# A macaron block with a selective scan: feed-forward stages dealt out in 128-token tiles, 3 or 4 beside each scan step

## The chip, the cores and the metric

The kernel runs on one core of a Trainium2 chip. A core has five engines with an instruction queue each, which meet through semaphores: TensorE (PE; its weight loads are shown as PEld), VectorE (DVE), ScalarE (ACT), GpSimd (POOL) and SyncE (SP), which here issues nearly all DMAs. The metric is device time in microseconds for one execution, as the median of several runs.

## What is computed

The input x has 4 sequences of 1024 tokens with 512 features, all float32. Three blocks follow each other, each with a layer normalisation in front of it and a residual around it: a feed-forward block (halved), a selective scan, and the same feed-forward block once more.

```python
x = x + 0.5 * ffn(layernorm(x))
x = x + attn(layernorm(x))
x = x + 0.5 * ffn(layernorm(x))

def ffn(x):                      # INTER = 1408
    g = einsum('th,ih->ti', x, gate_w) * gate_s
    u = einsum('th,ih->ti', x, up_w) * up_s
    return einsum('ti,hi->th', silu(g) * u, down_w) * down_s

def attn(x):                     # I = 1024 channels, N = 16 states, R = 128
    h, gate = split(einsum('blh,oh->bol', x, W_in), 2)
    h = silu(causal_conv4(h) + conv_b)
    ts, B, C = split(einsum('bil,oi->blo', h, Wx), [R, R + N])
    ts, B, C = rms(ts), rms(B), rms(C)
    delta = softplus(einsum('blr,ir->bil', ts, Wdt) + dt_bias)
    # s = exp(delta * A) * s + delta * B * h;  y = sum over N of s * C
    y = (scan(h, delta, A, B, C) + D * h) * silu(gate)
    return einsum('bil,hi->blh', y, Wout)
```

## The kernel before

The 4096 tokens are cut into 16 chunks of T = 256 tokens (J = 2 tiles of 128), four to a sequence. A chunk passes three stages: the first feed-forward pass (x to x1 in DRAM), the scan (x1 to x2 in DRAM), the second feed-forward pass (x2 to the output).

**The scan is the spine.** Step k scans chunk k. It has NI = 8 tiles of 128 channels with NS = 4 units each, 32 units in all. A unit (`unit`, L517) works on two halves of 2 x 256 columns: ACT computes the decay `da` into PSUM (L533), POOL the input `sb` (L536), DVE scans (L540) and multiplies by C into `pr` (L546), and ACT saves the last state (L545). One unit later PE adds up `pr` over the states into `yps` (`add_up`, L553). `da` has four buffers (two units), `sb` four (two units), `pr` three (three units). For every two channel tiles `head` (L448) makes delta with two small `dp` matmuls and ACT's `z`, `lg` (L461 to L469), POOL finishes it (`rest`, L472 to L476), and `rows` and `spread` send it through DRAM so that each row stands on 32 partitions.

**Everything else is background**, a list of `Work` pieces, each with a cost in PE columns, which `background(k)` (L656) makes for each step. The loop at L738 emits a unit, and after it as many pieces as keep the share of PE work done level with the share of DVE work; the pieces up to the next chunk's parameters are to be done HEAD = 10 units before the step's end. Weights come through a ring of 15 blocks of 256 KB, loaded up to LEAD = 13 blocks ahead in the order in which the pieces use them (`fetch`, L110). The queues' final order is a scheduler's; pinned instructions keep the order of the program.

In the background of step k stand: the gate half of W_in for chunk k (`gate`, L498: PE matmuls `gp`, ACT copies to `g`, one silu), the output projection of chunk k-1 (`tail`, L574: `op`, 32 records of 128x512), normalisation and transposes of chunk k+1 (`flips`), its conv half of W_in (`prep_conv`, L345: `hp`), its parameters (`prep_params`, L378: `sp`, `t`, `tsT`), and one **feed-forward pass** (class FFN, L212) over up to four tiles: 11 `gate_w` blocks, 11 `up_w` blocks, one `fo` group of 11 down matmuls for each 128-token tile. A float32 matmul shows as two records in the trace.

**What decides which tokens go where** is L638 to L643:

```python
    beside = {0: [(1, 1), (1, 2)]}
    for k in range(1, NCS):
        beside[k] = ([(1, k + 2)] if k + 2 < NCS else []) + ([(2, k - 2)] if k >= 2 else [])
    beside[NCS - 2].append((2, NCS - 3))
    beside[NCS - 1] = [(2, NCS - 2)]
```

An entry is (pass, chunk), so 256 tokens. Step 0 has two entries (512 tokens), step 1 one, steps 2 to 14 two, step 15 one. The first pass of chunk 0 is done alone in front (`start`), the second pass of chunk 15 alone at the end (`end`, L713): it loads x2 from DRAM after `tail` has stored it. Steps 14 and 15 are `late` (L645): their last entry is the chunk whose scan has just ended, so they do the tail first, and load and flip that chunk inside the step.

In front of the scan (L708 to L711) stand the first pass of chunk 0, the flips of step 0's pass and of chunk 0, `prep_conv(0)` with `gate(0)` woven in piece by piece, and the parameters with the first gate blocks of step 0's pass.

Of the kernel before, what the change touches and what calls it, by code (L numbers as in the profile page):

```python
# [13 lines left out]
P = 128  # L14
# [18 lines left out]
LEAD = 13  # L33
RING = 15
# [3 lines left out]
def macaron_kernel(ctx: ExitStack, tc: tile.TileContext, a: dict, out: bass.AP):  # L38
# [173 lines left out]
    class FFN:  # L212


        def __init__(self, name, halves):
            self.name, self.halves = name, halves
            self.n = len(halves) * T
            self.x = {}

        def load(self, h):  # L220
            if self.halves[h][0] == 2:
                settle()
                write()
            stage, c = self.halves[h]
            for j in range(J):
                r = c * J + j
                t = self.x[h, j] = p8.tile([P, H], F32, tag="xf", name=f"xf{self.name}_{h}_{j}")
                load(out=t, in_=a["x"][r * P : (r + 1) * P, :] if stage == 1 else x2[r])

        def stats(self, h, j):  # L230
            return stats(self.x[h, j], f"f{self.name}_{h}_{j}")

        def flip(self, xn, h, j):
            if not hasattr(self, "xT"):
                self.xT = p1.tile([P, KH, 2 * T], F32, tag="fxT", name=f"fxT{self.name}")
            o = h * T + j * P
            flip(xn, self.xT[:, :, o : o + P], f"f{self.name}_{h}_{j}")
# [42 lines left out]
        def down(self):  # L280
            parts = [(h, j) for h in range(len(self.halves)) for j in range(J)]
            wd = []

            def part(h, j):
                def emit(w=None):
                    wd.extend(w or [])
                    nm = f"{self.name}_{h}_{j}"
                    op = ps_m.tile([P, H], F32, tag="mm", name=f"fo{nm}")
                    o = h * T + j * P
                    for it in range(NF):  # L290
                        nc.tensor.matmul(  # L291
                            op, lhsT=self.hd[:, it, o : o + P], rhs=wd[it],
                            start=(it == 0), stop=(it == NF - 1),
                        )
                    x = self.x[h, j]
                    tmp = p2.tile([P, H], F32, tag="tmp", name=f"tmp{nm}")
                    stage, c = self.halves[h]
                    r = c * J + j
# [11 lines left out]
                return Work(NF * H, H, emit, [("down_w", it) for it in range(NF)] if h + j == 0 else ())  # L310

            r = [part(h, j) for h, j in parts]
# [261 lines left out]
    def tail(k):  # L574
# [3 lines left out]
        def part(j):  # L578
            def emit(w=None):
# [10 lines left out]
                store(x2[k * J + j], x)  # L590
# [15 lines left out]
    def flips(f, prep, halves=None):  # L606

        seq = []
        if f:
            seq = [(h, j) for h in (range(len(f.halves)) if halves is None else halves) for j in range(J)]  # L610
# [4 lines left out]
        def begin(n):  # L615
            if n < len(seq):
                h, j = seq[n]
                xn[n] = prep_stats(prep, j) if h is None else f.stats(h, j)
# [5 lines left out]
        def part(n):  # L624
            def emit():
                h, j = seq[n]
# [18 lines left out]
    def late(k):  # L645

        return k >= NCS - 2
# [208 lines left out]
```

## Time and profile before

| what | value |
|---|---|
| median of 3 runs | 3403.47 us (3403.05 to 3404.28) |
| the profiled execution: its time, its span | 3408.67 us, 3406.6 us |
| POOL L536, the scan's `sb` | 1024 x 1273 ns, 1280.4 us busy |
| DVE L540, the scan with a state | 1536 x 739 ns, 1060.1 us busy |
| ACT L533, the scan's `da` | 2048 x 470 ns, 901.3 us busy |
| DVE L546, `pr` | 1024 x 677 ns, 667.4 us busy |
| PE L243, `up_w` and `gate_w` | 1408 records each, 607.0 and 608.5 us busy |
| PE L291, `fo` | 1320 records, 587.4 us busy |
| PE L505 and L354, `gp` and `hp` | 1024 records each, 248.7 and 244.2 us busy |
| weight loads of gate, up, down | 198 each of 256 KB |
| DMA engines, mean busy share | 53.3% on the queue of SP's transfers |

Times are microseconds from the first instruction. The page's first part gives each engine's busy time; the second cuts the span into 40 slices, a digit being tenths of busy time, with the granted TensorE clock below. A stretch's row gives its length, and for each engine its busy time and (x) its instructions. A row of waits gives the waiting engine and instruction, what released it, and the total, the number and the longest of the waits. A busy engine is not an engine that sets the time: what matters is whether it has idle time, and what ended it.

### The profile page before, as it was taken

What the parts mean: (1) busy time and instruction counts of PE and PEld (TensorE: products, weight loads), DVE (VectorE), ACT (ScalarE), POOL (GpSimd) and SP (SyncE); (2) the same over time, 40 slices, a digit from 0 to 9 for tenths busy, and PEclk for the clock granted to TensorE, in tenths of its full rate; (3) what the DMA queues carried; (4) which work ended last, traced back from release to release, by engine and by line L of the source; (5) the groups of instructions that cost most, each with busy time, mean ns of one, the idle gap of its engine ahead of it and who ended that gap; (6) DMA issues with size and microseconds to landing.
All of it is one profiled execution on the core that took longest, in us unless ns stands there. A gap on an engine that the chain in (4) does not pass through costs nothing. (4 is left out here: it accounts for less than half of the span.)

```text
span 3406.6 us, 41741 instructions
## 1 busy us (share of the span) xinstructions
PE 3156.1 (93%) x12448; PEld 1609.4 (47%) x12448; DVE 2434.9 (71%) x4202; ACT 2001.4 (59%) x4395; POOL 2034.4 (60%) x1959
## 2 busy tenths in 40 slices
PE   8897676999999999999999999999999999989898
PEld 5534352544444454444445454444545444344445
DVE  1177686687868778786877778687786779757781
ACT  2446654756656575766657475765747576465551
POOL 1266655566665756666575666757566576655760
PEclk9997787999999999999999999999999999999899
DMA  6345454546555554656565465556546555643643
GB/s 201 97 125 138 136 137 123 147 129 185 146 163 156 155 156 117 189 138 171 142 171 161 118 180 137 161 142 171 163 124 177 130 161 142 186 114 100 192 136 105
DMA packets 286417, 504.59 MB, mean 148 GB/s; under 512 B 31984, under 2 KB 50160, under 8 KB 286192
## 3 DMA queue, kind: packets, MB, share of 16 engines
q1 hardware_dynamic: 284608, 501.47, 53.3%
q8 instruction: 100, 1.64, 0.2%
q14 instruction: 125, 1.02, 0.1%
q10 hardware_dynamic: 1584, 0.45, 0.1%
HBM read 442.56 MB, written 59.24 MB: 147 GB/s over the span
## 5 line engine op out<-in xcount | busy, mean ns | idle before, releaser
L536 POOL TENSOR_TENSOR sb<-rep,bc 128x512 f32<-128x512 f32 x1024 | 1280.4, 1273 | 466.0 <-DVE da L540 441.5
L540 DVE TENSOR_TENSOR_SCAN da<-da,state,sb 128x256 f32<-128x256 f32 x1536 | 1060.1, 739 | 263.5 <-ACT da L533 203.4
L533 ACT ACTIVATE da<-rep,a_w 128x256 f32<-128x256 f32 x2048 | 901.3, 470 | 266.2 <-DVE pr L546 249.4
L546 DVE TENSOR_TENSOR pr<-da,bc 128x512 f32<-128x512 f32 x1024 | 667.4, 677 | 77.8 <-ACT state L545 61.8
L243 PE MATMUL up_w<-fxT,w_up_w 128*128 128x512 f32 (+1 forms) x1408 | 607.0, 578 | 18.7 <-issue 13.7
L243 PE MATMUL gate_w<-fxT,w_gate_w 128*128 128x512 f32 (+1 forms) x1408 | 608.5, 577 | 9.6 <-ACT hd L257 4.8
L291 PE MATMUL fo<-w_down_w,hd 128*128 128x512 f32 x1320 | 587.4, 597 | 0.0
L556 PE MATMUL yps<-pr,fold 128*32 128x256 f32 x4096 | 386.6, 401 | 140.0 <-DVE pr L546 117.7
L545 ACT COPY state<-da 128x2 f32<-128x2 f32 x768 | 118.9, 161 | 498.6 <-DVE da L540 490.5
L243 PEld LDWEIGHTS up_w<-fxT,w_up_w 128*128 128x128 f32 x1408 | 260.5, 192 | 304.4 <-issue 288.3
L243 PEld LDWEIGHTS gate_w<-fxT,w_gate_w 128*128 128x128 f32 x1408 | 265.5, 193 | 283.8 <-issue 250.7
L540 DVE TENSOR_TENSOR_SCAN da<-da,sb 128x256 f32<-128x256 f32 x512 | 321.1, 679 | 96.5 <-ACT da L533 69.8
L291 PEld LDWEIGHTS fo<-w_down_w,hd 128*128 128x128 f32 x1320 | 244.6, 191 | 291.3 <-issue 282.7
L556 PEld LDWEIGHTS yps<-pr,fold 128*32 128x32 f32 x4096 | 105.0, 109 | 481.8 <-DVE pr L546 225.7
L472 POOL TENSOR_SCALAR e<-z 128x512 f32<-128x512 f32 x64 | 124.4, 1944 | 214.0 <-ACT z L468 204.9
L505 PE MATMUL gp<-mxT,w_W_in 128*128 128x256 f32 x1024 | 248.7, 392 | 1.9 <-ACT dd L467 1.1
L354 PE MATMUL hp<-mxT,w_W_in 128*128 128x259 f32 x1024 | 244.2, 388 | 5.7 <-issue 2.0
L585 PE MATMUL op<-w_Wout,u 128*128 128x512 f32 x512 | 234.6, 606 | 8.1 <-POOL sb L536 5.3
L365 DVE SCALAR_TENSOR_TENSOR u<-hp,conv_w,u 128x256 f32<-128x256 f32 x384 | 175.1, 473 | 71.2 <-ACT u L358 67.7
L354 PEld LDWEIGHTS hp<-mxT,w_W_in 128*128 128x128 f32 x1024 | 190.0, 190 | 62.3 <-issue 25.3
L505 PEld LDWEIGHTS gp<-mxT,w_W_in 128*128 128x128 f32 x1024 | 190.7, 192 | 57.2 <-issue 21.8
L566 POOL TENSOR_TENSOR u<-u,g 128x256 f32<-128x256 f32 x128 | 92.8, 730 | 196.4 <-DVE u L562 196.2
(114 smaller groups left out, 2744.5 us busy)
## 6 DMA issues: line engine op xcount, KB each, us to landing
rep<-row SPq DMA_DIRECT2D x512, 256.0 KB, 5.6
w_W_in<-in_W_in_dram SPq DMA_DIRECT2D x256, 256.0 KB, 3.1
w_gate_w<-in_gate_w_dram SPq DMA_DIRECT2D x198, 256.0 KB, 3.4
w_up_w<-in_up_w_dram SPq DMA_DIRECT2D x198, 256.0 KB, 3.0
w_down_w<-in_down_w_dram SPq DMA_DIRECT2D x198, 256.0 KB, 2.9
row<-dd SPq DMA_DIRECT2D x128, 256.0 KB, 4.5
w_Wout<-in_Wout_dram SPq DMA_DIRECT2D x128, 256.0 KB, 4.3
bc<-bcd SPq DMA_DIRECT2D x64, 256.0 KB, 4.7
```

The lines of the kernel that those rows point to most:

```text
L243: nc.tensor.matmul(o[:, : self.n], lhsT=w[:, k, :], rhs=self.xT[:, k, : self.n], start=(k == 0), stop=(k == KH - 1),)
L291: nc.tensor.matmul(op, lhsT=self.hd[:, it, o : o + P], rhs=wd[it], start=(it == 0), stop=(it == NF - 1),)
L354: nc.tensor.matmul(hp[:, : K - 1 + T], lhsT=w[:, kk, :], rhs=st[k]["xnT"][:, kk, :], start=(kk == 0), stop=(kk == KH - 1),)
L365: pin(nc.vector.scalar_tensor_tensor(u[:, i, :], hp[:, q : q + T], conv_w[:, i, q : q + 1], u[:, i, :], ALU.mult, ALU.add,))
L472: pin(nc.gpsimd.tensor_scalar(e, z, 1.0, 1.0, ALU.add, ALU.subtract))
L505: nc.tensor.matmul(gp[:, :T], lhsT=w[:, kk, :], rhs=st[k]["xnT"][:, kk, K - 1 :], start=(kk == 0), stop=(kk == KH - 1),)
L533: nc.scalar.activation(da[:, j, :], rep[:, h + j, 0, :], AF.Exp, scale=a_w[:, b0 + h + j, g : g + 1])
L536: nc.gpsimd.tensor_tensor(sb, rep[:, hs, 1, :], d["bc"][:, g : g + 1, :].to_broadcast([P, 2, T]), ALU.mult)
L540: nc.vector.tensor_tensor_scan(da[:, j, :], da[:, j, :], sb[:, j, :], 0.0 if first else state[:, b0 + h + j, g : g + 1], ALU.mult, ALU.add,)
L546: nc.vector.tensor_tensor(pr[:, hs, :], da, d["bc"][:, NS + g : NS + g + 1, :].to_broadcast([P, 2, T]), ALU.mult)
L556: nc.tensor.matmul(yp[j * Q : (j + 1) * Q, :], lhsT=fold, rhs=pr[:, j, :], start=(g == 0), stop=(g == NS - 1),)
L585: nc.tensor.matmul(op, lhsT=st[k]["u"][:, i, j * P : (j + 1) * P], rhs=wo[i], start=(i == 0), stop=(i == NI - 1),)
```

## The change

The unit in which feed-forward work is dealt out becomes one tile of 128 tokens instead of a chunk of 256. Six steps (`THREE`: 1, 3, 5, 8, 10, 12) get three tiles, so a gate or up matmul has 384 columns, and ten get four. Tiles of the first pass are dealt in order (4 in step 0, 3 in step 1, then 2 a step while there are any), the rest of a step is tiles of the second pass. A second-pass tile may be dealt to step k only if its chunk is at most k-2, so the special form of steps 14 and 15 goes. Beside the scan stand 58 tiles, where there were 60 (30 entries of two). Four tiles of the second pass are left (chunks 14 and 15): they form one pass behind the scan. The two of chunk 15 are used as `tail` leaves them in SBUF; x2 of that chunk is neither stored nor loaded. The other two are loaded in the middle of step 15, as is x1 for the last tail.

Apart from this the gate half of W_in for chunk 0 (`gate(0)`) leaves the front and is woven into step 0's first feed-forward blocks. `BEGUN` names the number 7 that stood in the code before.

```diff
+BEGUN = 7
+THREE = (1, 3, 5, 8, 10, 12)
...
-        def __init__(self, name, halves):
-            self.name, self.halves = name, halves
-            self.n = len(halves) * T
+        def __init__(self, name, tiles):
+            self.name, self.tiles = name, tiles
+            self.n = len(tiles) * P
             self.x = {}
 
-        def load(self, h):
-            if self.halves[h][0] == 2:
+        def load(self):
+            if any(stage == 2 for stage, _ in self.tiles):
                 settle()
                 write()
-            stage, c = self.halves[h]
-            for j in range(J):
-                r = c * J + j
-                t = self.x[h, j] = p8.tile([P, H], F32, tag="xf", name=f"xf{self.name}_{h}_{j}")
-                load(out=t, in_=a["x"][r * P : (r + 1) * P, :] if stage == 1 else x2[r])
-
-        def stats(self, h, j):
-            return stats(self.x[h, j], f"f{self.name}_{h}_{j}")
-
-        def flip(self, xn, h, j):
+            for t, (stage, r) in enumerate(self.tiles):
+                if t in self.x:
+                    continue
+                x = self.x[t] = p8.tile([P, H], F32, tag="xf", name=f"xf{self.name}_{t}")
+                load(out=x, in_=a["x"][r * P : (r + 1) * P, :] if stage == 1 else x2[r])
...
-            parts = [(h, j) for h in range(len(self.halves)) for j in range(J)]
...
+            def part(t):
...
-                store(x2[k * J + j], x)
+                if k + 1 < NCS:
+                    store(x2[k * J + j], x)
...
-    beside = {0: [(1, 1), (1, 2)]}
-    for k in range(1, NCS):
-        beside[k] = ([(1, k + 2)] if k + 2 < NCS else []) + ([(2, k - 2)] if k >= 2 else [])
-    beside[NCS - 2].append((2, NCS - 3))
-    beside[NCS - 1] = [(2, NCS - 2)]
+
+
+    first = [(1, r) for r in range(J, NCS * J)]
+    second = [(2, r) for r in range((NCS - 1) * J)]
+    beside = {}
+    for k in range(NCS):
+        m = 3 if k in THREE else 4
+        ones = min(len(first), 4 if k == 0 else 3 if k == 1 else 2)
+        twos = m - ones
+        beside[k] = [first.pop(0) for _ in range(ones)] + [second.pop(0) for _ in range(twos)]
+        done_1 = NCS * J - len(first)
+        assert done_1 >= min(NCS, k + 3) * J
+        assert all(r < (k - 1) * J for stage, r in beside[k] if stage == 2)
+    last = second + [(2, r) for r in range((NCS - 1) * J, NCS * J)]
     ffn = {k: FFN(k, beside[k]) for k in range(NCS)}
 
-    def late(k):
-
-        return k >= NCS - 2
-
-    def before(k):
-
-        f = ffn[k]
-        for h in range(len(f.halves)):
-            if not (late(k) and h == len(f.halves) - 1):
-                f.load(h)
+    def end_load():
+
+        for j in range(J):
+            end.x[len(end.tiles) - J + j] = st[NCS - 1]["xo", j]
+        end.load()
...
-                gate_0[7:] + f.up() + down[:J] + [then(prep_load, 1), turn[0]]
-                + weave(down[J:], turn[1:])[0] + [then(before, 1)]
+                weave(gate_0[BEGUN:] + f.up(), gate(0))[0] + down[:J]
+                + [then(prep_load, 1), turn[0]] + weave(down[J:], turn[1:])[0] + [then(ffn[1].load)]
...
-        if late(k):
-            parts += [out_of[0], out_of[1], then(f.load, len(f.halves) - 1)]
-            own = flips(f, None, [len(f.halves) - 1])
-            parts += [gates[0], own[0], gates[1], gates[2], own[1], gates[3], own[2]]
-            p = turn + gates[4:]
-        else:
-            parts += turn[:1]
-            p = [NOTHING] * 4 + gates + turn[1:] + out_of
-        p = p + conv
-        p = [p[n : n + 2] for n in range(0, len(p), 2)] + [[NOTHING]] * 4 + [[w] for w in params]
-        turn = []
-        if k + 1 < NCS:
-            turn = flips(ffn[k + 1], None, range(len(ffn[k + 1].halves) - late(k + 1)))
+        parts += turn[:1]
+        p = [NOTHING] * 4 + gates + turn[1:] + out_of + conv
         tiles = f.gate() + f.up()
+        p = [p[n : n + 2] for n in range(0, len(p), 2)]
+        p += [[NOTHING]] * 4 + [[w] for w in params]
+        turn = flips(ffn[k + 1], None) if k + 1 < NCS else []
         for n, w in enumerate(tiles):
             parts.append(w)
             for q in p[n : n + 1]:
                 parts += q
-            if n == NF and k + 1 < NCS:
-                parts.append(then(before, k + 1))
+            if n == len(tiles) - NF and k + 1 < NCS:
+                parts.append(then(ffn[k + 1].load))
+            if n == len(tiles) - NF and k + 1 == NCS:
+                parts.append(then(tail_load, k))
+                parts.append(then(end_load))
...
-    start = FFN("p", [(1, 0)])
+    start = FFN("p", [(1, r) for r in range(J)])
...
-    front += [turn_m[0], gate_0[2]] + turn_m[1:] + weave(prep_conv(0), gate(0))[0]
-    front += weave(gate_0[3:7], prep_params(0))[0]
+    front += [turn_m[0], gate_0[2]] + turn_m[1:] + prep_conv(0)
+    front += weave(gate_0[3:BEGUN], prep_params(0))[0]
     beside_scan = [background(k) for k in range(NCS)]
-    end = FFN("e", [(2, NCS - 1)])
-    back_end = [then(tail_load, NCS - 1)] + tail(NCS - 1) + [then(end.load, 0)]
-    back_end += flips(end, None) + end.gate() + end.up() + end.down()
+    end = FFN("e", last)
+    turn = flips(end, None)
+    back_end = tail(NCS - 1) + turn + end.gate() + end.up() + end.down()
...
-                if i == 0 and k and not late(k):
+                if i == 0 and k:
...
-        if not more or late(k + 1):
+        if not more:
```

## The prediction

> **What bounds the kernel now.** I read the page from above: busy shares, then the slices, then stretches cut at the first scan instruction (L540) of each step.
>
> ```profile
> PE 3156.1 (93%) x12448; PEld 1609.4 (47%) x12448; DVE 2434.9 (71%) x4202; ACT 2001.4 (59%) x4395; POOL 2034.4 (60%) x1959
> ...
> PE   8897676999999999999999999999999999989898
> ...
> PEclk9997787999999999999999999999999999999899
> ```
>
> TensorE (PE) is the fullest engine, but not evenly: slices 3 to 6 and the end have lower digits, and there the granted clock falls too. The answer by stretches (length, then busy time of PE, PEld, DVE, ACT, POOL, then clock and DMA) gives, row by row, the front, steps 0, 1, 3, 13, 14, 15, and the work behind the scan:
>
> ```profile
> 0.00:182.57 182.57, 161.17 (x555) 106.09 (x556) 31.33 (x70) 63.40 (x102) 33.19 (x55) 0.97 0.52 158
> 182.57:376.37 193.80, 152.75 (x631) 78.98 (x629) 140.13 (x252) 110.92 (x277) 123.96 (x115) 0.87 0.39 103
> 376.37:575.96 199.59, 137.36 (x604) 74.12 (x604) 149.98 (x261) 109.14 (x267) 121.36 (x119) 0.81 0.53 153
> 774.52:969.58 195.06, 190.35 (x755) 93.85 (x754) 153.13 (x262) 120.34 (x227) 126.12 (x122) 1.00 0.57 154
> 2742.71:2941.39 198.68, 193.64 (x753) 94.80 (x752) 152.12 (x257) 124.24 (x286) 126.00 (x117) 0.99 0.56 151
> 2941.39:3160.32 218.93, 200.79 (x752) 97.02 (x751) 151.89 (x258) 126.71 (x287) 124.83 (x116) 0.96 0.50 136
> 3160.32:3325.08 164.76, 142.39 (x631) 76.96 (x630) 133.83 (x218) 94.11 (x184) 105.12 (x91) 0.91 0.57 160
> 3325.08:3406.65 81.57, 66.78 (x248) 46.24 (x246) 12.09 (x24) 12.04 (x19) 7.81 (x11) 0.92 0.34 106
> ```
>
> Steps 2 to 13 last (2941.39 - 575.96) / 12 = 197.1 us each, and PE is idle for about 5 of them: PE-bound. Step 1 carries 256 feed-forward tokens instead of 512, leaves PE idle for 62 us, and yet lasts 199.6. So a step has a second limit, close to the first: the scan's own chain through ACT, POOL and DVE. The change is decided between these two. Where step 1 loses its time is in the waits of its stretch (total, times, longest):
>
> ```profile
> PE yps L556 <- DVE pr L546: 54.2, 20, 6.5
> ...
> ACT z L466 <- PE dp L461: 24.2, 2, 16.5
> DVE da L540 <- POOL sb L536: 15.2, 10, 2.9
> DVE da L540 <- ACT da L533: 14.0, 4, 10.9
> ```
>
> PE waits for the scan's products, while ACT once stands 16.5 us before `z`, because `dp` is queued behind 22 `fo` matmuls on PE; the scan's exponentials queue behind `z`.
>
> **PE's work in total does not change.** In the last group a 128x256 record takes (3382.46 - 3363.47) / 88 = 0.216 us (88 records of `up_we`, start to next group), and the 44 records of `foe` (128x512) take 19.05 us together, 0.433 each: time goes with width. A 128-token tile thus costs 176 gate and up records of 0.108 and 22 down records of 0.433, 19.0 + 9.5 = 28.6 us, wherever it stands. There are 18 weight passes before and after (front, 16 steps, end), so the 198 loads each of gate, up and down stay, as do 64 tiles. SP loses two x2 stores and two loads. Only idle and cold PE time can be won.
>
> **Part 1, the front (step 0's gate projections leave it).** 64 records of `gp` x 0.216 = 13.8 us, in a stretch where PE is nearly always busy. Against it: `sp` waited 4.5 us for the silu of `u` at 128.1, with `gp` 7 as cover; that cover goes (1.7). DVE's three taps (1.42) stay under a conv block's 1.75 on PE. From the `dp` matmuls at 147.0 to the first scan at 182.6 lie 35.6 us of latency; in the changed issue order PE has 7 feed-forward blocks of 3.46 and 6 `gp` of 1.73 for it, 34.6, where it had 10.5 x 3.46 = 36.3. **-12** (-14 to -9).
>
> **Part 2, step 0.** The same 13.8 us come in here, where PE runs almost without idle from 182.6 to 258.9; after that it has a gap of 11 us and smaller ones. Upper end 14, lower end 0; DVE idles 53 us in this step, so part is absorbed: **+8**.
>
> **Part 3, step 1** gets a third tile, 28.6 us of PE into 62 us idle. At the rates above (0.77 per `yps` unit, from step 3's rest) the records started in this stretch are 111 us of work, but PE is busy 137: the rest is cold clock[...]. The added work fills gaps; the scan stays the limit. **-6** (-15 to +8).
>
> **Part 4, steps 3, 5, 8, 10, 12** lose one tile. Lower end: 190.35 - 28.6 - 0.9 (transposes) = 160.9, plus step 3's 4.7 idle, 166. Upper end: step 1's 199.6. I take it by halves. The first half of step 3 (774.5 to 873.7) is 99.2 us with PE busy 98.1; twelve narrower gate and up blocks take 12 x 0.87 = 10.4 away: 88. But step 1's first half, with PE busy only 74, took 92.7: I take 93. The second half is 95.9 with PE 92.3 and DVE 80.0; PE falls by 10 x 0.87 + 9.5 + 0.9 to 73, DVE by about 3 (narrower `hd`, one `tmp`, one statistic) to 77. So DVE leads there; step 1's second half had 71.6 of DVE in 106.9. In the changed order `dp_2` again stands behind 22 `fo` matmuls (9.5 us plus its own 1.0, while the four `da` buffers let ACT run two units, 7.5 us, ahead), so some 4 to 11 us of that stall come back, besides waits for `sb`. I take 14.5 of stalls on 77, which is 91.5. Sum 184.5 against 197, five times: **-62** (-155 to +13).
>
> [...]The row: where PE idles 5 us of a step the clock is 1.00; 18 us (step 14) 0.96; 62 us (step 1) 0.81. [...]So relieving PE makes it slower. [...]By the row of step 14, 0.96: 168, below the 184.5 that I have for the scan, so nothing on the path. I take the row: PE is left about 24 us of idle, nearer to step 14 than to step 1.[...]
>
> **Part 5, step 14.** Its own way of working (tail first, the last half flipped inside the step) goes, and its PE order becomes that of step 13: 218.9 - 197 = **-22** (-24 to -18).
>
> **Part 6, step 15** has 512 tokens instead of 256. Records started there are 98 us of work at the rates above and 24.6 of `yps`; add two tiles, 57.2, and take away 24 records of `op` (10.4) that now stand behind the scan: about 169. With some 6 idle: 175, while DVE has 139 and a fifth more in waits would be 167. **+10** (+4 to +18).
>
> **Part 7, behind the scan.** Now: last scan at 3325.1, `op` done at 3330.9, gate from 3342.8, end of `foe` 3401.5, 5.1 for the last output. After: pr and yps 1.4, all of `op` 13.9 (none under the scan now), then add, statistics, POOL's three small ones, `xn`, transposes and copy: 6.9, because x2 is no longer stored and loaded again (between L589 at 3331 and the statistics at 3336.5 lay 5.5). Two tiles are flipped meanwhile. Then 2 x 57.2 = 114.3 for 512 tokens, 1.8 for a cold start, 5.1: 143.4 against 81.6. **+62** (+58 to +65). The new loads at step 15's middle wait on SP for two x2 stores, with weight loads queued behind; 13 blocks of lead, at 1.7 us or more each, hide that.
>
> **Sum**: -12 + 8 - 6 - 62 - 22 + 10 + 62 = -22. Against the profiled execution's own 3408.7 (span 3406.6) that is 3386.5; the runs' median lies 5.2 below that execution: **3381**. Without Part 4 the sum is +40, so it turns where a lightened step saves 40 / 5 = 8 us.
>
> **Rivals.** (a) *PE stays the bound*: the lightened steps come down to 167. For it: in steps 2 to 13 DVE's waits are mostly for PE (`fo`, `yps`, and ACT behind `gate_w`). Against it: steps 0 and 1. 40 - 5 x 30 = -110: 3294. (b) *The scan's own pace takes over*, and the end is paid in full. Place: `dp_2` behind `fo` at the end of each lightened step with the scan's `da` behind `z`, and a cold PE after each gap. Price: a lightened step at 195, saving 2. For it: both light steps of the trace last 194 and 200. It decides from a saving below 8 on: 40 - 10 = +30, 3433, slower. (c) *The gate projections land wholly in step 0*: Part 2 at +14 and Part 1 at -9 give 9 more, 3390; this alone changes no sign.
>
> **How the numbers follow.** A measurement of this kernel can tell about 0.2%, 6.8 us, from no change. Forecast (saving 8 to 18 per lightened step, 3330 to 3403, best 3381): 0.48. Rival a (over 18): 0.15. Rival b (under 8): 0.37. Savings between 6.6 and 9.4 are within 0.2%: 0.09, taken from both sides; faster 0.56, slower 0.35. The forecast's own range with the other parts' bounds is 3335 to 3410; the range for 8 in 10 takes in half of rival a and rival b with step 1 unrelieved: 3325 to 3440.
>
> **What would show it.** Right: steps 3, 5, 8, 10, 12 at 178 to 190, with PE idle near 20 and a clock of 0.93 to 0.97, step 14 at 197, step 15 near 175, 143 behind the last scan, front near 171. Wrong: lightened steps at 194 or more with a clock near 0.8 and long waits of `z` for `dp` (rival b), or at 170 with PE full (rival a). It is also wrong if step 0 and the front together gain or lose over 15 us, or if the last pass, which has nothing beside it, waits for weights.

## The result: 3.7% slower

| | before | after |
|---|---|---|
| median | 3403.55 us (3403.05 to 3404.28, 4 runs) | 3530.4 us (3528.5 to 3532.7, 4 runs) |
| ratio | | 1.0373, interval 1.0355 to 1.0391 |
| profiled execution, its span | 3408.67 us, 3406.6 us | 3530.08 us, 3528.3 us |

The forecast was 3381, the range 3325 to 3440: wrong in sign, and outside the range. The page of the changed kernel, in the lines shown of before:

```profile
PE 3201.5 (91%) x12448; PEld 1618.3 (46%) x12448; DVE 2444.5 (69%) x4202; ACT 2005.6 (57%) x4401; POOL 2030.7 (58%) x1959
...
PE   8897688999889998999998799998999799999999
...
PEclk9998898999989998999999899999999799999999
```

All engines but POOL are busy a little longer, with the same number of instructions on PE and DVE: the work is the same and the time is 122 us longer. The dips in PE at the end are gone and those at the front are fewer; new ones stand in the middle. The stretches, cut as before at the first scan of each step (length, busy time of PE, PEld, DVE, ACT, POOL, clock, DMA): front, steps 0, 1, 3, 4, 5, 7, 8, 12, 14, 15, and behind the scan.

```profile
0.00:169.19 169.19, 144.75 (x509) 96.17 (x510) 29.10 (x68) 59.77 (x98) 33.11 (x55) 0.97 0.52 159
169.19:384.27 215.08, 172.84 (x681) 89.30 (x679) 144.72 (x257) 118.40 (x287) 124.87 (x118) 0.89 0.38 102
384.27:574.12 189.85, 151.24 (x626) 74.20 (x626) 152.42 (x261) 110.33 (x266) 121.65 (x119) 0.89 0.58 162
773.57:980.76 207.19, 178.53 (x767) 94.62 (x765) 153.88 (x262) 124.17 (x237) 130.06 (x125) 0.93 0.57 160
980.76:1176.91 196.15, 187.14 (x718) 92.07 (x719) 144.28 (x258) 118.85 (x277) 120.89 (x116) 0.98 0.50 137
1176.91:1383.06 206.15, 179.24 (x769) 94.77 (x767) 153.78 (x262) 129.95 (x300) 131.34 (x126) 0.95 0.58 161
1582.21:1777.31 195.10, 190.83 (x753) 93.84 (x752) 152.61 (x259) 119.00 (x225) 124.97 (x119) 1.00 0.55 153
1777.31:1995.14 217.83, 185.25 (x769) 98.01 (x767) 146.98 (x263) 129.99 (x299) 131.53 (x127) 0.91 0.55 154
2598.33:2814.81 216.48, 182.64 (x769) 95.83 (x767) 146.63 (x264) 129.88 (x299) 131.48 (x127) 0.93 0.56 155
3016.78:3213.67 196.89, 191.13 (x757) 94.23 (x756) 153.45 (x261) 125.68 (x290) 127.09 (x122) 1.00 0.56 155
3213.67:3376.21 162.54, 159.89 (x601) 70.69 (x599) 135.86 (x215) 97.80 (x182) 106.43 (x91) 1.00 0.52 143
3376.21:3528.30 152.09, 143.83 (x375) 63.42 (x374) 18.75 (x29) 17.67 (x21) 11.04 (x14) 0.99 0.25 78
```

Row by row against before: front -13.4, step 0 +21.3, step 1 -9.7, step 14 -22.0, step 15 -2.2, behind the scan +70.5: together +44. The lightened steps 3, 5, 8, 10, 12, which were to save 62, last 207, 206, 218, 206 and 216, +69 in sum; steps 4, 6, 9, 11, 13 behind them add 7. Steps 2 and 7 give 1 more. That is the 122 of the span.

What a lightened step looks like inside is seen when it is cut in two behind the fourth channel tile. First the halves of step 5 before, then after:

```profile
1166.46:1267.46 101.00, 99.12 (x406) 51.59 (x405) 73.38 (x123) 73.89 (x157) 61.32 (x57) 1.00 0.62 177
1267.46:1364.11 96.65, 92.77 (x355) 43.02 (x354) 80.06 (x139) 52.10 (x134) 66.54 (x67) 1.00 0.49 131
```

```profile
1176.91:1282.01 105.10, 96.83 (x427) 55.57 (x425) 75.44 (x125) 75.65 (x161) 63.69 (x58) 0.98 0.63 180
1282.01:1383.06 101.05, 82.41 (x342) 39.20 (x342) 78.34 (x137) 54.30 (x140) 67.65 (x69) 0.92 0.54 142
```

The missing tile did leave: PE is 2 and 10 us less busy, and the records of the second half cost more at a clock of 0.92 (a `yps` record 0.12 us of busy time, before 0.08). But both halves became longer. In the second, neither PE (82 of 101) nor DVE (78 of 101) is full. What DVE waits for is in the waits of step 8, the longest of the lightened steps (total, times, longest wait):

```profile
DVE u L560 <- PE yps L554: 18.9, 4, 10.7
DVE da L538 <- ACT da L531: 13.2, 6, 5.0
DVE pr L544 <- ACT state L543: 8.1, 9, 4.5
DVE da L538 <- POOL sb L534: 6.3, 5, 2.6
```

DVE waits for all three partners of the scan in turn. No single wait took the place of the one removed. Late weights are not the cause: none of PE's waits in step 8 is for a DMA.

### The profile page after: what moved, and what is told of

Same layout as the page of the kernel before. It is cut to its first block, busy times and chain, and to the rows that moved or that the text cites. A ratio compares the mean times of both kernels' runs of the same rounds, so it can differ in the third digit from the quotient of the medians.

```text
span 3528.3 us, 41712 instructions
## 1 busy us (share of the span) xinstructions
PE 3201.5 (91%) x12448; PEld 1618.3 (46%) x12448; DVE 2444.5 (69%) x4202; ACT 2005.6 (57%) x4401; POOL 2030.7 (58%) x1959
## 5 line engine op out<-in xcount | busy, mean ns | idle before, releaser
L244 PE MATMUL gate_w<-fxT,w_gate_w 128*128 128x512 f32 (+1 forms) x1408 | 600.2, 570 | 16.8 <-ACT fxT L209 6.9
L244 PE MATMUL up_w<-fxT,w_up_w 128*128 128x512 f32 (+1 forms) x1408 | 584.4, 561 | 17.6 <-issue 17.6
L554 PE MATMUL yps<-pr,fold 128*32 128x256 f32 x4096 | 411.4, 410 | 194.6 <-DVE pr L544 154.1
L290 PE MATMUL fo<-w_down_w,hd 128*128 128x512 f32 x1276 | 568.2, 598 | 0.0
L290 PEld LDWEIGHTS fo<-w_down_w,hd 128*128 128x128 f32 x1276 | 237.5, 191 | 284.4 <-issue 277.4
L503 PE MATMUL gp<-mxT,w_W_in 128*128 128x256 f32 x1024 | 256.5, 396 | 1.7 <-ACT hd L258 0.9
L564 POOL TENSOR_TENSOR u<-u,g 128x256 f32<-128x256 f32 x128 | 92.7, 729 | 277.1 <-DVE u L560 246.3
L470 POOL TENSOR_SCALAR e<-z 128x512 f32<-128x512 f32 x64 | 124.3, 1942 | 206.6 <-ACT z L466 150.4
```

What stands on the lines that cost most here:

```text
L244: nc.tensor.matmul(o[:, : self.n], lhsT=w[:, k, :], rhs=self.xT[:, k, : self.n], start=(k == 0), stop=(k == KH - 1),)
L290: nc.tensor.matmul(op, lhsT=self.hd[:, it, t * P : (t + 1) * P], rhs=wd[it], start=(it == 0), stop=(it == NF - 1),)
L470: pin(nc.gpsimd.tensor_scalar(e, z, 1.0, 1.0, ALU.add, ALU.subtract))
L503: nc.tensor.matmul(gp[:, :T], lhsT=w[:, kk, :], rhs=st[k]["xnT"][:, kk, K - 1 :], start=(kk == 0), stop=(kk == KH - 1),)
L554: nc.tensor.matmul(yp[j * Q : (j + 1) * Q, :], lhsT=fold, rhs=pr[:, j, :], start=(g == 0), stop=(g == NS - 1),)
```

## Experiments

The letters in the expectations: theory A, the scan's own in-order chain through ACT, POOL, DVE and PE sets a light step, so that less PE work does not shorten it (A1: the gating and the sum of `u` at a channel tile's end stand badly in it; A2: the next chunk's `head` at the end of a lightened step does); theory B, the idle PE loses its clock (in the trace of before 1.00 in step 3 with PE idle for 5 us, 0.81 in step 1 with 62); theory D, the gate projections in step 0 stand ahead of the chain to chunk 1. Theories E (the border between a full and a light step costs) and F (whole groups of down matmuls stand in the way) came later. All lengths of steps are of the profiled execution. Each batch ran on one chip, beside the kernel before, whose median was 3402.7 to 3407.7; single runs are therefore compared to some 5 us.

**More work, less time.** The changed kernel, with a fourth tile of the second pass done once more in the five lightened steps and its result not stored:

```diff
+    for k in THREE[1:]:
+        beside[k].append((3, 2 * (k - 2)))
...
```

> The changed kernel with a fourth tile in steps 3, 5, 8, 10 and 12: a tile of the second pass that was done before is worked on once more and not stored, so 5 x 28.6 = 143 us of TensorE work are added. Theory A (a lightened step is ruled by the scan's own chain and by engines that wait on each other in turn; an even, full TensorE is what makes a step 197 us): the five steps and their successors come back to 197 us each, 79 us less than in the changed kernel, 3450 in all, although more is computed. Theory B (TensorE's cold clock alone makes the lightened steps long): the clock comes back to 1.00 in them, which gives back only the some 10 us of each that cold matmuls cost, but the added work then stands on the path: 3530 - 50 + 143, over 3600. Theory C (some other part, such as the last pass, sets the loss): no gain, 3530 or more.

3457.9 us: 143 us of PE work more (an estimate, five tiles of the 28.6 us that a tile has by the trace of before; PE was busy for 3262.6 us in place of 3201.5), 72 us less time. Steps 3, 5 and 8:

```profile
776.23:971.27 195.04, 190.34 (x755) 93.84 (x754) 153.12 (x262) 120.32 (x227) 125.99 (x122) 1.00 0.57 154
1168.40:1367.64 199.24, 193.50 (x759) 94.93 (x758) 153.44 (x262) 126.05 (x290) 127.76 (x123) 0.99 0.58 153
1760.07:1957.14 197.07, 190.66 (x757) 94.10 (x756) 146.02 (x262) 125.35 (x288) 127.21 (x123) 1.00 0.57 154
```

So 72 us come with the lightening, and go when the work is put back. That is theory A's forecast (3450); B's was over 3600.

**The curve of tiles.** Four tiles everywhere, but 3 in steps 1 and 5, 2 in step 9, 1 in step 13 (one 128-token tile of the second pass is left out of the computation):

```diff
-THREE = (1, 3, 5, 8, 10, 12)
+FEWER = {1: 3, 5: 3, 9: 2, 13: 1}
...
```

> The changed kernel with four tiles in every step but 1 (three), 5 (three), 9 (two) and 13 (one); where no tile is due, one that was done before is worked on again and not stored, and one second-pass tile (128 tokens) is left out. Steps with no lighter neighbour should last 197. Theory A: a light step and the one behind it together last about as long for three, two and one tiles, 390 to 410 us: the scan's side has a pace of its own near 195 to 200. If TensorE's work were the bound, each tile less would take 28.6 us: 365, 337, 308. Theory B: the pair grows longer with fewer tiles, as the clock falls: above 405 for one tile.

Steps 5, 9 and 13:

```profile
1164.97:1369.89 204.92, 177.68 (x769) 93.89 (x767) 153.88 (x262) 129.84 (x300) 131.38 (x126) 0.96 0.59 162
1956.93:2170.96 214.03, 162.93 (x749) 95.48 (x747) 151.01 (x262) 124.92 (x299) 129.78 (x126) 0.86 0.56 157
2761.81:2973.99 212.18, 141.94 (x725) 81.63 (x723) 148.90 (x260) 123.67 (x299) 128.12 (x124) 0.79 0.56 159
```

PE is idle for 27, 51 and 70 us in them. With three tiles gone, 86 us of PE work, step 13 is 13.5 us longer than before (198.7), not shorter. With the step behind it each makes 404, 414 and 413 us. PE's work is not the bound; A's 390 to 410 is missed for two tiles and for one, and B's "above 405 for one tile" holds. So this run does not rule out the cold clock.

**The light steps at the end.**

```diff
-THREE = (1, 3, 5, 8, 10, 12)
+FEWER = {1: 3, 13: 3, 14: 2, 15: 2}
...
```

> The same 58 tiles beside the scan, but the lightening is put together at the end: steps 2 to 12 have four tiles, 13 three, 14 and 15 two. Theory A: steps 2 to 12 at 197; 13 with 14 some 400 to 405; step 15, which prepares nothing for a next step, 155 to 162. In all 3530 - 79 + 8 - 4, about 3455. If the number of lightened tiles counted and not where they are: 3530 as before.

3474.5 us. Steps 3 to 12 are back at 195 to 199; 13, 14, 15 and the rest last 205.9, 210.2, 180.9, 133.8. Step 15, with two tiles in place of four, is 18 us longer than in the changed kernel, and what is behind the scan 18 us shorter, where PE has 82 records fewer. Steps 13 and 14 lose. A's forecast (3455, with 400 to 405 for 13 and 14 and 155 to 162 for 15) is missed, and so is 3530 for a loss that goes by the number of tiles alone.

**The clock.** The changed kernel with zero-weight fold matmuls in channel tiles 4 to 7 of the five steps. These are the matmuls that sum `pr` into `yps`, with weights of zero (`nought`), so they add nothing:

```diff
+    nought = const.tile([P, Q], F32, name="nought")
+    nc.gpsimd.memset(nought, 0.0)
...
+        if g and k in THREE[1:] and i in (4, 5, 6, 7):
+            for _ in range(3):
+                for j in range(S):
+                    nc.tensor.matmul(
+                        yp[j * Q : (j + 1) * Q, :], lhsT=nought, rhs=st[k]["bc"][:, j, :],
+                        start=False, stop=False,
+                    )
```

> The changed kernel with a filler on TensorE in steps 3, 5, 8, 10 and 12: in each unit of their tiles 4 to 7 except the first of a tile, three sets of the fold's matmuls with weights of zero on operands that lie ready, before the unit's real fold; they add nothing to the result. 12 units a step, some 1.6 us each, near 19 us of work a step that otherwise would be waiting. Theory B[...]: the clock of the five steps rises from 0.91 to 0.95 to about 1.00, and each gets 5 to 12 us shorter, 3470 to 3505 in all. Theory A (waits in order of the queues, clock of little matter): no gain, or the added work makes them longer: 3525 to 3570.

3463.0 us. The five steps last 192.5, 197.3, 197.1, 195.0, 197.1 at 0.98 to 0.99, which is B's side. Steps 5 and 6:

```profile
1166.98:1364.30 197.32, 183.10 (x961) 99.38 (x963) 152.49 (x261) 124.31 (x289) 125.32 (x121) 0.99 0.57 159
1364.30:1564.78 200.48, 192.55 (x822) 95.02 (x823) 153.32 (x261) 127.91 (x292) 128.51 (x123) 1.00 0.52 147
```

But the scheduler also put the last `head` later here: its `z` stands 11 or 12 of ACT's `da` instructions (4 make a unit) later than in the changed kernel, and so behind the step's border. With one set in place of three:

> f1_warm with one set of zero matmuls a unit instead of three, 0.5 us a unit, 6 us a step. Theory B: if so little keeps the clock up, the steps get shorter than in f1_warm, where the filler itself stood on TensorE's path in tile 7: 188 to 196 each, 3430 to 3460 in all. If it is too little to keep the clock (below 0.97 in tiles 5 to 7), the time lies between f1_warm and the changed kernel, 3465 to 3520.

3532.4 us at 0.93 to 0.95, slower than either forecast: 96 such records a step held neither clock nor time, 288 held both (granted clock over the execution 0.960 and 0.979; 0.956 in the changed kernel). The order alone, with no added matmul:

```diff
+                late = k in THREE[1:] and i == NI - 1
...
-                if i % 2 == 1 and g == 1 and k2 < NCS:
+                if i % 2 == 1 and g == (3 if late else 1) and k2 < NCS:
```

> The filler of f1_warm also moved instructions: in its lightened steps ACT's z for the next chunk's head 2 no longer stands before the exponentials of tile 7's unit 2, so that a head moved out of the step. Here the changed kernel has no filler, but in the lightened steps that head is emitted two units later, and ACT's order at the step's end becomes like that of f1_warm. If the place of the head was the cause (theory A2), the five steps fall to about 197 and the whole to 3460 to 3480. If the cold clock was (theory B), they stay at 203 to 218, 3510 to 3535.

3510.9 us, clocks still 0.93 to 0.95: the time that was set down for B. But this edit does not give quite the order of the run with 288 records. Here `z` moves by 8 `da` instructions in four steps and by 3 in step 3, and stays before the border. So this later place (A2) is worth 19 of the 67 us. The held clock (B) and the rest of the head's way have the other 48, about 10 a step; no run parts these two. A step with its successor comes no lower than before: steps 3 and 4 take 392.6 (before 391.9), 5 and 6 take 397.8 (394.6). In the kernel before, the same matmuls in steps 0, 1 and 15:

> The kernel before with the filler of f1_warm where its trace shows a low clock: tiles 4 to 7 of steps 0 and 1, tiles 1, 2 and 5 of step 15. Theory B: step 0 from 194 to 185 to 190, step 1 from 200 to 185 to 192, step 15 by 2 to 5 less: 3375 to 3395, faster than both kernels. Theory A: 3403 to 3420.

3409.9, ratio 1.0020 (1.0012 to 1.0028): step 0 at a clock of 0.95 in place of 0.87 gains 0.5 us, step 1 at 0.89 in place of 0.81 gains 5, step 15 and the end lose 5. Over the execution the clock rose to 0.979 from 0.969 to 0.971, and that bought nothing there, against B's 3375 to 3395.

**The end of a channel tile (A1).** The multiplication by the gate on POOL pinned in its place, and then also the sum into `u` on DVE put off by two units:

```diff
-        nc.gpsimd.tensor_tensor(u, u, g_all[:, i, :], ALU.mult)
+        pin(nc.gpsimd.tensor_tensor(u, u, g_all[:, i, :], ALU.mult))
...
+            whole.append([2, lambda: pin(nc.vector.scalar_tensor_tensor(
+                u, u, d_w[:, i : i + 1], yp, ALU.mult, ALU.add))])
```

> The changed kernel, with POOL's product of u and g held in the program's order, behind the units of the tile four further on, where the scheduler had moved it up to just behind DVE's sum of its own tile. In the changed kernel POOL waits 246 us for that sum, and the scan's sb stands behind it. Theory A1 (light steps are long because POOL's queue waits for DVE, DVE for TensorE, and the scan for POOL): POOL's wait for DVE u goes, the lightened steps fall from 206 to 218 to 190 to 200, 3440 to 3480 in all. Theory B (cold clock): less than 15 us are gained.

> As the run before, and DVE's sum of u and yps, which ends a tile, stands two units later in DVE's queue, so that TensorE may lag by three units instead of one. In the changed kernel DVE waits 171 us for yps here, 14 to 19 us in each lightened step. Theory A1: these waits go too, lightened steps at 180 to 192, and below the full ones: 3400 to 3450 in all. Theory B: the cold clock keeps them near 200, 3490 to 3530.

3527.2 and 3516.9 us, against A1's 3440 to 3480 and 3400 to 3450. Pinning does nothing. Putting off brings the lightened steps to 200 to 205, but the full ones to 197 to 205. The same edits in the kernel before:

> The same two edits in the kernel before. Its steps 2 to 13 are bound by TensorE and gain nothing (197); steps 0, 1, 14 and 15, where TensorE has idle time of 41, 62, 18 and 22 us, could get shorter by 5 to 10 each under theory A1: 3370 to 3395. Under theory B or if the waits lie elsewhere: 3400 to 3410.

3452.0 us, a loss that neither forecast had: steps 2 to 13 pay 1 to 5 us each. Here, what served the steps in which PE idled for 25 to 34 us harmed those in which it idled for 5 to 10.

**Gate projections of chunk 0.** Only that part of the change, in the kernel before:

```diff
-                gate_0[7:] + f.up() + down[:J] + [then(prep_load, 1), turn[0]]
+                weave(gate_0[7:] + f.up(), gate(0))[0] + down[:J] + [then(prep_load, 1), turn[0]]
...
-    front += [turn_m[0], gate_0[2]] + turn_m[1:] + weave(prep_conv(0), gate(0))[0]
+    front += [turn_m[0], gate_0[2]] + turn_m[1:] + prep_conv(0)
```

> The kernel before with one part of the change: step 0's gate projections leave the front and stand within step 0. In the changed kernel the front became 13 us shorter and step 0 21 us longer, step 1 10 shorter, but there step 0 also flips and starts a pass of three tiles. My prediction's terms for this part (-12 and +8) give 3399; theory A, with the 14 us of TensorE work fully on step 0's path, gives 3403 to 3411.

3420.5, ratio 1.0038 (1.0024 to 1.0052). Front -13.0, step 0 +25.7, step 1 -0.6: 12 us lost for 13.8 us of PE work moved, more than either forecast (3399; 3403 to 3411). Behind step 0's down projections instead, which needs a second buffer for the normalised chunk, for which the weight ring gives up room (`both` interleaves two lists):

```diff
-LEAD = 13
-RING = 15
+LEAD = 11
+RING = 13
...
-            st[k]["xnT"] = p1.tile([P, KH, K - 1 + T], F32, tag="xnT", name=f"mxT{k}")
+            st[k]["xnT"] = p2.tile([P, KH, K - 1 + T], F32, tag="xnT", name=f"mxT{k}")
...
-                + weave(prep_conv(1), flips(ffn[1], None))[0] + [NOTHING] + params
+                + both(weave(prep_conv(1), flips(ffn[1], None))[0], gate(0)) + [NOTHING] + params
...
```

> Why did e4_gate0_only lose 26 us in step 0 for 13.8 us of TensorE? Theory D: the pieces stood at the head of a chain: the pass of step 0 makes x1 of chunk 1, which the same step normalises, convolves and turns into chunk 1's parameters. Here the gate projections of chunk 0 stand behind the down projections, between chunk 1's conv blocks (with a second buffer for the normalised chunk, and the weight ring at 13 blocks with 11 of lead to make room). Theory D: front 13 us shorter as in e4, step 0 at 194 to 200 instead of 219: 3392 to 3403. If any place in step 0 costs as much: 3415 to 3425.

3395.7, ratio 0.9981 (0.9973 to 0.9988), 0.2% faster than the kernel before. Its control has the buffers and the ring alone:

> The kernel before with two buffers for the normalised and transposed chunk, and 13 ring blocks with a lead of 11 instead of 15 and 13, nothing else: the control for the run with the first gate projections behind step 0's down projections (3395.7, 0.9981). If the second buffer (or the ring) alone made that gain: 3394 to 3398, with step 14 at about 211 and steps 0 and 1 at 193.8 and 199.6. If the gate's place made it: 3401 to 3406, front and steps 0 and 1 together at 576 instead of 570. In between: each has a share, step 14's 7.5 us from the buffers and the 6 us at the front from the place.

3398.1, ratio 0.9970 (0.9957 to 0.9982). The rows of the control's steps 0, 1 and 14, then those of front, 0 and 1 with the gate behind:

```profile
182.78:379.54 196.76, 150.00 (x615) 77.74 (x613) 140.37 (x251) 109.96 (x275) 123.98 (x115) 0.85 0.39 101
379.54:569.36 189.82, 138.67 (x620) 75.32 (x620) 148.95 (x261) 107.05 (x266) 121.49 (x119) 0.83 0.58 157
...
2938.42:3150.03 211.61, 198.21 (x753) 96.00 (x752) 151.87 (x257) 123.71 (x285) 124.70 (x116) 0.97 0.54 142
```

```profile
0.00:165.91 165.91, 144.68 (x491) 92.40 (x492) 31.33 (x70) 58.46 (x93) 33.12 (x55) 0.98 0.53 159
165.91:380.31 214.40, 165.16 (x679) 90.16 (x677) 140.55 (x252) 115.60 (x285) 124.27 (x115) 0.85 0.39 101
380.31:570.00 189.69, 139.21 (x620) 76.29 (x620) 149.10 (x260) 107.00 (x266) 121.32 (x119) 0.83 0.57 158
```

Up to step 2 they make 569.4 and 570.0. So the gain is that of the buffers and the ring (9.8 us in step 1 and 7.3 in step 14, while step 0 loses 3), not of the place. The place is worth 12 us between its two positions: woven into the gate and up blocks it delays what leads to chunk 1 (D), behind the down projections it costs nothing and brings nothing. Which of buffer and ring makes it was not separated.

**A floor, or only a cold clock?** The curve of tiles once more, with zero-weight matmuls in tiles 4 to 7 of step 5 and in all tiles of steps 9 and 13 (the same tile is left out; none is in fact done twice):

```diff
+WARM = {5: (4, 5, 6, 7), 9: range(8), 13: range(8)}
...
```

> The run with steps 5, 9 and 13 at three, two and one tiles, once more (one 128-token tile of the second pass is left out, further tiles are done twice and the second result is not stored), now with zero-weight fold matmuls added beside the scan: in tiles 4 to 7 of step 5, in all tiles of steps 9 and 13. Without them these steps took 204.9, 214.0 and 212.2 us at clocks 0.96, 0.86, 0.79. The rated PE work with them is about 188, 178 and 150 us. Theory A (the scan's own chain through ACT, POOL, DVE and PE sets the floor): the clock comes back to 0.95 or more, but steps 9 and 13 stay at 188 to 200, though PE is idle 15 to 40 us. Theory B (only the cold clock made light steps long): step 9 comes down to 178 to 186 and step 13 to 155 to 178. If neither the clock nor the length changes in 9 and 13, the additions are too small and nothing is told.

Steps 5, 9, 13: 196.7, 201.0, 209.5 at 0.99, 0.96, 0.89, PE idle for 14, 18, 45 us. Step 9 is the cleaner test: with the clock back at 0.96, from 0.86, it gains 13 us and stops at 201, where B had 178 to 186. In step 13 the clock was not brought back; B's 155 to 178 is missed there too. A's 188 to 200 is missed in both (they are longer, and step 13 is colder than A said). Next, the lightened steps side by side:

```diff
-THREE = (1, 3, 5, 8, 10, 12)
+THREE = (1, 8, 9, 10, 11, 12)
```

> The changed kernel with its lightened steps side by side: 1, 8, 9, 10, 11, 12 instead of 1, 3, 5, 8, 10, 12. Theory E (what costs is the border from a full step to a light one, the scan units and head pieces carried over it): step 8 stays at 206 to 218, but 9 to 12 fall to 184 to 192, as the forecast had them, and the whole is 3440 to 3475. Theory A or B (a light step is slow by itself, by the scan's own chain and the cold clock): steps 8 to 12 are each 200 to 220, steps 2 to 7 and 13 stay at 194 to 200, and the whole is 3510 to 3550.

3486.9 us, 43 less than with the steps apart. Steps 8 to 13:

```profile
1754.01:1960.77 206.76, 187.41 (x789) 99.17 (x787) 145.23 (x260) 128.83 (x297) 129.97 (x123) 0.96 0.58 160
1960.77:2159.82 199.05, 177.30 (x725) 93.98 (x726) 150.71 (x258) 122.29 (x288) 123.28 (x118) 0.94 0.52 144
2159.82:2357.69 197.87, 177.79 (x731) 94.08 (x730) 150.57 (x258) 121.76 (x287) 124.52 (x119) 0.95 0.55 151
2357.69:2557.63 199.94, 176.06 (x729) 92.59 (x728) 150.95 (x258) 113.88 (x224) 125.77 (x120) 0.94 0.54 150
2557.63:2771.64 214.01, 181.14 (x718) 92.01 (x716) 145.61 (x262) 119.38 (x284) 126.40 (x123) 0.91 0.53 144
2771.64:2973.33 201.69, 191.38 (x722) 93.28 (x723) 152.31 (x259) 120.02 (x279) 121.84 (x118) 0.97 0.50 137
```

Neither theory's numbers hold. A light step between light ones lasts 198 to 200, like a full one: no saving, no loss. This block of six rows is 34 us longer than before's steps 8 to 13 (1219.3 - 1185.3), while the changed kernel, with five pairs of borders, loses 76. Of the 34, steps 8 and 12 have 27. They are the ends of the block, but they also scan the first chunks of a sequence, and the run does not part the two. For the border speak steps 3, 5 and 10 of the changed kernel, which start no sequence and are 8 to 12 us longer than before when they stand alone.

**Lumps.** Each group of 11 down matmuls beside the scan in two pieces of 6 and 5:

```diff
-        w, turn = weave(turn[1:2] + f.down(), [NOTHING] + turn[2:])
+        w, turn = weave(turn[1:2] + f.down((0, 6, NF)), by)
...
```

> The changed kernel with each group of 11 down matmuls (fo, 22 records, 9.5 us) beside the scan dealt out as two pieces of 6 and 5, so that dp, yps and the parameters need not stand behind a whole group. Theory F (the work beside a light step is dealt out unevenly: tiles in which PE is full and the scan waits alternate with tiles in which PE waits for the scan and gets cold, and the whole groups of fo are the lumps): steps 3, 5, 8, 10, 12 fall from 206 to 218 to 198 to 207 each, the whole is 3465 to 3505. Theory A (the in-order chain of the scan's own instructions is the floor at about 197 to 200 and the borders cost the rest, whatever the lumps): 3515 to 3535.

> The kernel before with the same split of the down matmuls, nothing else: what the split is worth where PE is nearly full. Theory F: full steps stay at 194 to 199, since PE has no idle time to win, the whole is 3395 to 3410. If the finer pieces change the order for the worse (weights and the scan's sums exchange places more often): 3410 to 3440.

3526.6 (1.0367, 1.0351 to 1.0382) and 3406.2 (1.0010, 1.0003 to 1.0017): nothing gained. In step 8 of the first `z` still waits once for `dp`, 16.0 us, since PE runs half group after half group from 1947 to 1981, with one gap of 3 us, and three of them pass while `z` waits. F fails as it was put.

**The scan's pace.** Two tiles beside each of steps 4 to 11 (11 tiles of the second pass are left out), zero-weight matmuls in 8 to 11:

```diff
+FEWER = {1: 3} | {k: 2 for k in range(4, 12)}
+WARM = {k: range(8) for k in range(8, 12)}
...
```

> A measurement of the scan's own pace: in steps 4 to 11 only two tiles of feed-forward work stand beside the scan (the second-pass tiles that these steps would have done are left out), with zero-weight fold matmuls in all tiles of steps 8 to 11 and none in 4 to 7. The rated PE work of such a step is about 140 us, with the zero-weight matmuls about 178. Theory A (floor by the scan's own chain): the inner steps 5, 6, 7 last 195 to 210 at a clock of 0.8 to 0.9, and 9, 10, 11 still 193 to 202 at 0.95 or more. Theory B (cold clock): 5 to 7 at 190 to 205, 9 to 11 at 180 to 188. Theory F (no floor near 197; bunching and borders): 5 to 7 at 175 to 190, and 9 to 11 at 180 to 188.

Steps 4, 5 and 6 (none added), then 9 and 10 (added):

```profile
968.26:1167.78 199.52, 164.00 (x763) 97.46 (x761) 141.90 (x257) 122.83 (x296) 126.78 (x119) 0.91 0.58 163
1167.78:1377.21 209.43, 162.56 (x702) 94.84 (x703) 148.23 (x256) 116.98 (x284) 122.18 (x115) 0.85 0.50 140
1377.21:1585.33 208.12, 164.19 (x705) 94.68 (x704) 148.15 (x255) 119.31 (x286) 122.22 (x115) 0.85 0.50 141
...
1992.75:2198.29 205.54, 182.70 (x1283) 108.51 (x1283) 148.37 (x256) 119.08 (x288) 122.53 (x115) 0.95 0.53 143
2198.29:2403.67 205.38, 184.53 (x1281) 109.98 (x1280) 148.56 (x255) 117.87 (x285) 122.50 (x115) 0.93 0.52 143
```

Steps 7 and 11 last 199.1 and 206.6. With two of four tiles gone, in steps among their like, a step lasts 199 to 209; a warmer PE (0.93 to 0.95 in steps 8 to 11, in place of 0.85 to 0.91 in 4 to 7) leaves it at 205 to 208. That is A's side, though 9 to 11 are longer than A's 193 to 202; B's and F's 180 to 188 are ruled out. With two tiles PE does not set the step. The border does not explain these steps: step 4, at the border, is short (199.5), and 5 and 6 inside are 10 us longer than the steps with three tiles inside a block. No engine is full either. In step 6 (208 us) DVE, the busiest of the scan's engines, has 148, and its waits are

```profile
DVE da L542 <- ACT da L535: 29.0, 8, 11.6
DVE pr L548 <- ACT state L547: 11.7, 9, 3.2
DVE u L571 <- PE yps L565: 8.0, 7, 3.9
DVE hd L278 <- PE up_w L247: 5.6, 5, 2.6
DVE da L542 <- POOL sb L538: 5.3, 5, 2.1
```

Its longest, 11.6 us, comes from `z` on ACT, 15.8 us behind a `dp` that PE has after two groups of `fo`. The floor is thus not the scan's arithmetic. I read it as the scan together with the other pieces that stand in the queues' fixed orders; no run tried these steps in another order, so this is not shown.

## Why the prediction was wrong

**Part 4 is the step that failed**: "I take 14.5 of stalls on 77, which is 91.5. Sum 184.5 against 197, five times: -62". Measured 206 to 218, +69, and +76 with the steps behind them. Of the 144 us between the sum of -22 and the +122 of the spans this part is 131. Even its upper end (199.6, +13) was too low. It failed in both halves:

- First half, taken as 93 because step 1's took 92.7 with PE busy for 74. Step 5's took 105.1 with PE busy for 96.8. Step 1 was the wrong row: its first channel tile had no gate blocks beside it and took 15.5 us, where a lightened step's has them and took 27.8. Narrower blocks did not free this half either, since the loop dealt further pieces into it (64 `hp` records in place of 48): PE was relieved by 2 us, not 10.
- Second half, taken as 77 of DVE and 14.5 of stalls. DVE had 78.3; the stalls were 22.7. The work was right, the stalls were not, and they came from several waits: DVE waited 8.0 us for ACT's `da`, 5.5 for `state`, 5.3 for `yps` and 6.3 for POOL (a wait across the stretch's edge counts in full). `z` waited for `dp` only 4.9 us at most.

The thought behind it was wrong too: that the length is the larger of PE's work and the scan's work plus some stalls. The runs with 3, 2 and 1 tiles show a length that does not fall with PE's work at all. Rival b had this mechanism in part (the scan's pace takes over, at 195), and its 3433 was nearest. Its place, the long wait of `z` for `dp`, was wrong too: the longest in the changed kernel is 9.7 us. It too lacked the border. The working has a slip besides: by its own terms savings of 8 to 18 us a step give 3353 to 3403, not 3330 to 3403.

**The border** stood nowhere in the prediction. Side by side, lightened steps inside the block take 198 to 200, no more than full ones; apart, each with its successor takes 7 to 24 us more, 15 on average. Some 4 of the 15 are the later place of the head, up to 10 the held clock and the rest of the head's way. In a lightened step 280 `yps` records and five heads run, in the next 232 and three; inside the block it is 256 and four, as in full steps. So what a full step leaves over is caught up in the light one. Why steps 8 and 12, the first of a sequence, lose most (20 us) was not found.

**The clock.** Part 4 took the clock of step 14 (0.96, PE idle for 18 us) and not that of step 1 (0.81, 62 us). Measured: 0.91 to 0.95 over the step, with PE idle for 25 to 34 us. The estimate of idle time (24) was near; the clock lay between the two rows. Step 1's clock would make 199 us of the 160.9 us of PE work (160.9 / 0.81, an estimate), nearer to the measured 206 to 218 than 184.5. Within step 1 it was not even: in the trace of before it was 1.00 from 396.9 to 482.2 us and 0.50 from 499.3 to 530.0, where gaps of 2.1 to 6.5 us stand before `yps`. A set of eight `yps` records took 1.66 to 1.67 us there, and 0.64 us in step 3 at 1.00. In the last pass, `gate_we` records began 0.43 us apart at 0.50 and 0.216 apart at 1.00. But the cold clock is at most part of the cause: with zero-weight matmuls at 0.98 to 0.99 the steps came to 192 to 197, and no further.

**Part 2** (+8, bounds 0 to 14; measured +21.3). It counted PE time. In step 0 all pieces of the pass lead to x1 of chunk 1 and so to its parameters, so that gate pieces between them delay the chain to the next chunk. Alone they made 25.7 us there, and behind the down projections they cost no more than they took from the front.

**Right**: Part 1 (-12, measured -13.4), Part 3 (-6; -9.7), Part 5 (-22; -22.0), and, taken together, Parts 6 and 7 (72; 68). Alone both lie outside their bounds: Part 7 was +62 and came out at +70.5, Part 6 was +10 and came out at -2.2. With PE idle for 2.6 us at full clock, step 15 took 162.5, not 175. Work was put on the wrong side of the last scan: 22 `fo` records of step 15's pass, 10 us, run behind it. Full steps otherwise add 8, of which 7 stand behind lightened steps.

## What to carry to other kernels

Where two engines are both near a step's length, taking work off one may buy nothing. Run the kernel with that work simply left out and see whether the step gets shorter; here such a run would have told before any rescheduling. An even load can be worth more than a small one: light and full steps in turn cost 15 us a pair (76 in all), the same light steps in a row 34 us in all. That holds here for three tiles of four; with two, steps in a row took 199 to 209. When a trace offers a "light" step as a row, compare what stands in its queues tile by tile before its length is used.

## What the runs showed of the hardware

- A fourth tile, done once more in each of the five lightened steps, brought their granted clock from 0.91 to 0.95 up to 0.99 to 1.00, and the time of the kernel down by 72 us (clock and order together), though PE was busy for 61 us more.
- To hold the clock took much here: with 96 zero-weight records in a step it was 0.93 to 0.95 (0.960 over the execution, 0.956 without them), with 288 it was 0.98 to 0.99 (0.979).
- A higher clock in itself brought little: in the kernel before, step 0 gained 0.5 us from 0.87 to 0.95, step 1 only 5 us from 0.81 to 0.89, and the whole gained nothing (3409.9 us at 0.979 over the execution, 3402.7 at 0.969 to 0.971); with two tiles beside the scan, steps 5 and 6 took 209 and 208 us at 0.85, steps 9 and 10 took 206 and 205 at 0.95 and 0.93.
